# A two-layer graph attention kernel: layer 1's masks on ScalarE in two operations, and missing parts added by VectorE straight from PSUM

## The chip, the cores and the metric

The kernel runs on one core of one Trainium2 chip. The metric is the device time of one execution in microseconds. Five engines work side by side, each through its own queue in program order, and wait for one another through semaphores: TensorE (PE; its weight loads are shown as PEld), VectorE (DVE), ScalarE (ACT), GpSimd (POOL) and SyncE (SP, which here only issues DMAs).

## The reference

`x` has 6250 rows of 768 numbers; there are 100,000 edges, sorted by destination, and every node has a loop to itself. Two graph attention layers (4 heads of 64, then 1 head of 256) and a two-layer MLP stand behind a layer norm and a ReLU, with a residual:

```python
def gat_conv(x, src, dst, W, a_src, a_dst, bias, heads):
    h = (x @ W).reshape(n, heads, -1)
    alpha_s = (h * a_src[None]).sum(-1)
    alpha_d = (h * a_dst[None]).sum(-1)
    e = leaky_relu(alpha_s[src] + alpha_d[dst], 0.2)
    e = exp(e - segment_max(e, dst)[dst])
    alpha = e / (segment_sum(e, dst)[dst] + 1e-16)
    out = segment_sum(h[src] * alpha[:, :, None], dst)
    return out.reshape(n, -1) + bias
...
h = relu(gat_conv(relu(layernorm(x)), ..., heads=4))
h = relu(gat_conv(h, ..., heads=1))
return x + relu(h @ Wm1 + bm1) @ Wm2 + bm2
```

## The kernel before

The first stage (up to about 190 us) computes layer 1's features for 49 tiles of 128 nodes. Each tile stays in SBUF (`kept[t]`) and is stored as rows of `table[1]` in DRAM. Then layer 1 and layer 2 each run `layer_edges` over the edges, in `NG` = 196 groups `g` of 4 tiles of 128 edges; two tiles make a pair, 8 tiles a unit `u`, 16 tiles a node tile `t` (four groups, `j` = 0 to 3). The whole order of instructions on each engine is written out by hand in the loop over `g` (a manual schedule); there is no planner.

For a pair, GpSimd gathers the 128 source rows of each tile by an indirect DMA (L714) into a buffer `G` (24 buffers of one pair), 8 groups ahead of its use in program order. VectorE then multiplies the pair's weights (L792, L802) and, in layer 1, scales the gathered rows to `hw` (L804, 8 buffers); TensorE multiplies them by a one-hot matrix `hot` (L742, VectorE) and sums into `o_ps` (L816, one PSUM buffer for each unit). In layer 2 VectorE builds the weighted one-hot `hw` instead (L799). VectorE joins the units' sums (`acc`, L827), ScalarE copies their quarters (`sum`, L836), and the node's steps (normalise, turn, product with W2; L1010 to L1071) follow some groups later.

The weights need, for every edge, a factor of its destination node. For that a mask of 128 x 1024 bf16 is made for each unit: mask[p, e] is 1 where edge e's destination has the number p within its window of 128 nodes, else 0. `drow` holds the numbers modulo 128 on every partition; `pidx` holds p. TensorE multiplies the mask by the factors (`meet`, L760, into the one PSUM buffer `e_parts`), ScalarE copies the result (`parts_sb`, L772), and VectorE adds its three parts (`join`, L779). In layer 1 `make_mask` (L731) makes the mask on VectorE and SyncE writes it to DRAM (`mask_d`, L733); layer 2 reads it back. `make_mask` is called in the groups with odd `j`, for a unit about 5 units further on; `meet(t + 2)` is called at `j` = 0; `parts_out(t + 2)` at `j` = 3. There are 6 mask buffers.

Some pairs (30 in layer 1, one in each six or seven groups; 10 in layer 2) are gathered ahead, while the table that they read is not complete yet; sources that are not there yet are read as row 0. Such pairs (`SOON`, `NEXT`) are kept in DRAM and come back into a `G` buffer by a SyncE DMA (`soon_back`, L321). What is missing in them is added later: VectorE builds one-hot matrices of the missing sources, one for each missing node tile (`soon_hits`, L334, 3 buffers; in one to three parts, each one group before its product), TensorE multiplies them by the tiles in SBUF (`soon_missing`, L347; all into one PSUM buffer with the tag `missing`), ScalarE copies the sum to SBUF (`soon_out`, L352, tile `soon_m`), and VectorE multiplies the row by a 0/1 flag and adds the copy (`soon_whole`, L357). A pair has two tiles k; for a pair used in group `at`, the last part of its second tile is multiplied in group `at - 2`, copied in `at - 1`, and both rows are made whole in `at`. In layer 2 the same is done by `next_hits`, `next_missing` (L410), `next_out` (L416, tile `next_m`) and `next_whole` (L421): the products in `at - 6` and `at - 2`, the copies one group later, both additions in `at`.

Within a group the order is: the first pair, the node's steps, `gather_up`, `make_hot`, at fitting `j` `meet`, `ahead` or `make_mask`, then the actions on the early rows in the order of `SOON_ORDER`, then the second pair, the steps again, and at `j` = 3 `parts_out` and `join`.

Of the kernel before, what the change touches and what calls it, by code (L numbers as in the profile page):

```python
# [10 lines left out]
F32 = mybir.dt.float32  # L11
BF16 = mybir.dt.bfloat16
I32 = mybir.dt.int32
AF = mybir.ActivationFunctionType
ALU = mybir.AluOpType
AX = mybir.AxisListType

P = 128
# [44 lines left out]
def portions(there):  # L63

    n = -(-(NT - there) // PART)
    cuts = [there + (NT - there) * k // n for k in range(n + 1)]
    return list(zip(cuts, cuts[1:]))


SOON_DOES = {}  # L70
for i, at in enumerate(SOON_GROUP):
    todo = [(2 * i + t, k) for t in range(2) for k in range(len(portions(SOON[i])))]
    for j, (k, part) in enumerate(todo):
        g = at - 1 - len(todo) + j
        SOON_DOES.setdefault(g - 1, []).append(("hits", k, part))
        SOON_DOES.setdefault(g, []).append(("missing", k, part))
        if part == len(portions(SOON[i])) - 1:
            SOON_DOES.setdefault(g + 1, []).append(("out", k, part))
            SOON_DOES.setdefault(at, []).append(("whole", k, part))
    SOON_DOES.setdefault(max(at - 5 - len(todo), 0), []).append(("sources", i, 0))  # L80
SOON_ORDER = ("whole", "out", "missing", "hits", "sources")

UP_AT = {4 * u + 11: u for u in range(NU - 16)}
UP_AT.update(zip((338, 341, 344, 348, 351, 355, 358, 362, 366, 370, 373, 377, 380, 384), range(NU - 16, NU - 2)))
# [9 lines left out]
def kernel(  # L94
# [21 lines left out]
    nc = tc.nc  # L116
# [3 lines left out]
    def pool(name, bufs, **kw):  # L120
        return ctx.enter_context(tc.tile_pool(name=name, bufs=bufs, **kw))

    const = pool("const", 1)
# [4 lines left out]
    def bcast(src, n, off=0):  # L128
# [9 lines left out]
                   allow_small_or_imprecise_dtypes=True)  # L138
    pidx = const.tile([P, 1], F32, name="pidx")
    nc.gpsimd.iota(pidx, pattern=[[0, 1]], base=0, channel_multiplier=1,  # L140
                   allow_small_or_imprecise_dtypes=True)
    nid = const.tile([P, NT], F32, name="nid")
    nc.gpsimd.iota(nid, pattern=[[P, NT]], base=0, channel_multiplier=1,
                   allow_small_or_imprecise_dtypes=True)
    wbase = const.tile([P, NU, 2 * TPG], F32, name="wbase")
    nc.gpsimd.iota(wbase, pattern=[[64, NU], [0, 2 * TPG]], base=-32, channel_multiplier=0,
                   allow_small_or_imprecise_dtypes=True)
# [4 lines left out]
    nc.vector.tensor_copy(nid_ps, nid)  # L152
    eps_c = const.tile([P, 1], F32, name="eps_c")
    nc.vector.memset(eps_c, EPS)
    idle = const.tile([P, 4 * P], BF16, name="idle")
    nc.vector.memset(idle, 0.0)
    ones_c = const.tile([P, 1], F32, name="ones_c")
# [19 lines left out]
    TW = {1: RW[1] + 8, 2: RW[2] + 1}  # L177
# [113 lines left out]
    soon_i = const.tile([P, len(SOON), 2], I32, name="soon_i")  # L291
    soon_ok = const.tile([P, len(SOON), 2], F32, name="soon_ok")
    soon_d = dram.tile([len(SOON), P, 2 * TW[1]], F32, name="soon_d")
    soon_G, soon_of, soon_p, soon_hit, soon_m = {}, {}, {}, {}, {}
    soon_pair = {i: pair for pair, i in SOON_AT.items()}
    renewed = set()

# [49 lines left out]
            nc.tensor.matmul(soon_p[k], hit[:, T - a], kept[T], start=(T == there),  # L347
                             stop=(T == NT - 1))

    def soon_out(pool, k):  # L350
        soon_m[k] = pool.tile([P, TW[1]], F32, name="soon_m", bufs=3)
        nc.scalar.activation(soon_m[k], soon_p.pop(k), AF.Copy)  # L352

    def soon_whole(G, k):
        i, t = divmod(k, 2)
        row = G[soon_pair[i]][:, t]
        nc.vector.scalar_tensor_tensor(row, row, soon_ok[:, i, t:t + 1], soon_m.pop(k),  # L357
                                       ALU.mult, ALU.add)

    next_i = const.tile([P, len(NEXT), 2], I32, name="next_i")  # L360
    next_ok = const.tile([P, len(NEXT), 2], F32, name="next_ok")
    next_d = dram.tile([len(NEXT), P, 2, TW[2]], F32, name="next_d")
    next_G, next_of, next_p, next_hit, next_m = {}, {}, {}, {}, {}
    next_pair = {i: pair for pair, i in NEXT_AT.items()}

    def next_places(i):
# [24 lines left out]
    def next_sources(pool, i):  # L391

        next_of[i] = pool.tile([P, 2 * P], I32, name="next_of", bufs=1)
        nc.sync.dma_start(next_of[i], bcast(src_rows, 2 * P, 2 * P * next_pair[i]))

    def next_hits(pool, i, t):

        m = NT - NEXT[i]
        next_hit[i, t] = pool.tile([P, NT - NEXT_FROM, P], F32, name="next_hit", bufs=2)
        nc.vector.tensor_tensor(  # L400
            next_hit[i, t][:, :m],
            next_of[i][:, t * P:(t + 1) * P].unsqueeze(1).to_broadcast([P, m, P]),
            nid_ps[:, NEXT[i]:].unsqueeze(2).to_broadcast([P, m, P]), ALU.is_equal)

    def next_missing(i, t):

        there, hit = NEXT[i], next_hit.pop((i, t))
        next_p[i, t] = ps.tile([P, TW[2]], F32, name="missing2", tag="missing", bufs=1)
        for T in range(there, NT):
            nc.tensor.matmul(next_p[i, t], hit[:, T - there], kept[T][:, :TW[2]], start=(T == there),  # L410
                             stop=(T == NT - 1))

    def next_out(pool, i, t):

        next_m[i, t] = pool.tile([P, TW[2]], F32, name="next_m", bufs=2)
        nc.scalar.activation(next_m[i, t], next_p.pop((i, t)), AF.Copy)  # L416

    def next_whole(G, i, t):

        row = G[next_pair[i]][:, t]  # L420
        nc.vector.scalar_tensor_tensor(row, row, next_ok[:, i, t:t + 1], next_m.pop((i, t)),  # L421
                                       ALU.mult, ALU.add)

    def next_steps(g, pool, sm, G):

        for i, at in enumerate(NEXT_GROUP):
            if g == at - 10:
                next_sources(pool, i)
            for t in range(2):
                first = at - 6 + 4 * t  # L430
                if g == first - 1:
                    next_hits(pool, i, t)
                if g == first:
                    next_missing(i, t)
                if g == first + 1:
                    next_out(sm, i, t)
                if g == at:
                    next_whole(G, i, t)

    mask_d = dram.tile([NU * P, 8 * P], BF16, name="mask_d")  # L440
# [216 lines left out]
    drow, mask = {}, {}  # L657
# [15 lines left out]
    def fetch_mask(u):  # L673

        if u < NU:
            b = (min(8 * u + 8, LAST) - 8 * u) * P
            mask[u] = maskp.tile([P, 8 * P], BF16, name="mask")
            nc.sync.dma_start(mask[u][:, :b], mask_d[u * P:(u + 1) * P, :b])

    def layer_edges(layer, H, node, pre, matched, pre_pool):  # L680
# [4 lines left out]
        with tc.tile_pool(name=f"eg{layer}", bufs=6) as eg, \  # L685
# [33 lines left out]
            def both(u):  # L719
                return tiles(2 * u)[0], TPG + tiles(2 * u + 1)[-1] + 1  # L720

            def make_mask(u):

                if not 0 <= u < NU:
                    return
                if layer == 2:
                    return fetch_mask(u + 1)
                a, b = (t * P for t in both(u))
                mask[u] = maskp.tile([P, 8 * P], BF16, name="mask")
                at = u % 2 * 8 * P  # L730
                nc.vector.tensor_scalar(mask[u][:, a:b], drow[u // 2][:, at + a:at + b], pidx, None,  # L731
                                        ALU.is_equal)
                nc.sync.dma_start(mask_d[u * P:(u + 1) * P, a:b], mask[u][:, a:b])  # L733

            def make_hot(g):
# [138 lines left out]
            if layer == 1:  # L874
                for r in range(3):
                    fetch_rows(r)
                soon_away(0)
                fetch_rows(3)
                for u in range(4):
                    make_mask(u)  # L880
            else:
                next_away()
# [46 lines left out]
            for g in range(NG):  # L929
                t, j = divmod(g, 4)  # L930
# [21 lines left out]
                if j == 0:  # L952
                    if layer == 1:
                        fetch_rows(t + 4)
                    node.prefetch(t)
                    if layer == 2 or t == 0:
                        meet(t + 1)
                    if layer == 1 and t > 0:
                        meet(t + 2)
                elif j == (2 if t < NT - 1 else 1):  # L960
                    node.ahead(t)
                elif j % 2 and (layer == 2 or t > 0):
                    make_mask((g + (11 if layer == 1 else 7)) // 2)
# [7 lines left out]
                if layer == 1:  # L971
                    for what, k, part in sorted(SOON_DOES.get(g, ()),
                                                key=lambda d: (SOON_ORDER.index(d[0]), d[1], d[2])):
                        if what == "whole":
                            soon_whole(G, k)
                        elif what == "out":
                            soon_out(sm, k)
                        elif what == "missing":
                            soon_missing(k, part)
                        elif what == "hits":  # L980
                            soon_hits(pre_pool, k, part)
                        else:
                            soon_sources(pre_pool, k)
                else:
                    next_steps(g, pre_pool, sm, G)
# [545 lines left out]
```

## Time and profile before

| what | value |
|---|---|
| median of 3 runs | 2706.55 us (2704.31 to 2711.71) |
| profiled execution | 2711.53 us, of which 2709.7 are the span from its first to its last instruction |
| TensorE, weight loads | 1897.7 and 1425.3 us busy |
| VectorE | 1495.4 us busy |
| ScalarE | 454.4 us busy |
| GpSimd | 1534.3 us busy |
| mean granted TensorE clock | 0.821 |

Times inside the span count from its start. A group of instructions is told by its line in the kernel, engine, operation and tile (out<-in), with the number of instructions, the busy time and the mean duration; the idle time of the engine just before these instructions follows, with what released them. "Issue" is time in which the engine waited for nothing that the trace shows; "remote" and "another core or an unknown queue" are waits without a releaser in the trace. In a timeline, the columns are the start in us, the duration in us, the engine, the line, the operation, out<-in with its shape, how many instructions were merged, and in brackets the idle time before and its releaser.

### The profile page before, as it was taken

The page shows a single profiled execution, that of the slowest core. Times are in us where ns is not written, and L with a number is a line of the kernel's source. Part 1 is how long each engine was busy: PE and PEld are TensorE (multiplying, and loading weights), DVE is VectorE, ACT ScalarE, POOL GpSimd, SP SyncE. Part 2 cuts the span into 40 slices and gives each one's busy share as a digit, 9 for nine tenths or more (in the row PEclk, how much of TensorE's full clock was granted, in tenths as well). Part 3 has the DMA queues.
Part 4 walks back from the last instruction along what each step waited for, and adds up shares of the span by engine and source line. Part 5 has one row for each costly group of instructions (what it writes and reads, how often), then busy time and mean ns, then how long its engine had stood idle before and what let it go on. Part 6 is the DMA issues. An engine that isn't in the chain of part 4 may idle for free.

```text
span 2709.7 us, 28790 instructions
## 1 busy us (share of the span) xinstructions
PE 1897.7 (70%) x8572; PEld 1425.3 (53%) x8574; DVE 1495.4 (55%) x4344; ACT 454.4 (17%) x1415; POOL 1534.3 (57%) x1669
## 2 busy tenths in 40 slices
PE   9772486888796877866656436777777667777668
PEld 7651365666575655645435224555554445545445
DVE  8542476667675756565666424454544445454445
ACT  6540011111111111101102101111111111111112
POOL 5457455455554545354562466666666666666661
PEclk9985698899897888887788657888878878877779
DMA  9877344444544444343552554455545555554442
GB/s 358 247 240 240 115 140 136 125 133 141 146 128 123 135 113 139 109 128 106 147 155 68 144 148 116 140 155 154 157 146 155 155 149 155 153 158 147 143 146 92
DMA packets 174907, 405.46 MB, mean 150 GB/s; under 512 B 37192, under 2 KB 61983, under 8 KB 174743
## 3 DMA queue, kind: packets, MB, share of 16 engines
q0 software_dynamic: 75040, 210.90, 29.5%
q1 hardware_dynamic: 98332, 191.14, 20.9%
q10 hardware_dynamic: 1370, 1.48, 0.2%
q8 instruction: 72, 1.18, 0.2%
q14 instruction: 93, 0.75, 0.1%
HBM read 334.24 MB, written 69.14 MB: 149 GB/s over the span
## 4 chain that ended last, share of the span: by engine, by line
PE 37%; issue 21%; another core or an unknown queue 15%; DVE 13%; POOL 3%; DMA 2%; ACT 1%; DVEq 0%; ACTq 0%; POOLq 0%
PE o_ps L816 17%; PE missing L347 9%; PE y_ps L1186 5%; POOL G L714 3%; DVE hw L799 2%; PE missing L410 2%; DMA G<-table,src_i 2%; DVE hw L804 2%; DVE hot L742 2%; DVE soon_hit L334 1%; DVE iota_ps L792 1%; PE tp L1176 1%; DVE acc L827 1%; PE e_parts L760 1%
## 5 line engine op out<-in xcount | busy, mean ns | idle before, releaser
L714 POOL DMA_INDIRECT G<-table,src_i x1484 | 1416.8, 955 | 1053.2 <-issue 380.7
L816 PE MATMUL o_ps<-G,hw 128*128 128x258 f32 x1564 | 487.1, 446 | 177.0 <-issue 130.3
L347 PE MATMUL missing<-kept,soon_hit 128*128 128x268 f32 x1648 | 463.3, 432 | 207.7 <-ACT soon_m L352 130.5
L347 PEld LDWEIGHTS missing<-kept,soon_hit 128*128 128x128 f32 x1648 | 342.6, 212 | 301.0 <-ACT soon_m L352 138.0
L816 PEld LDWEIGHTS o_ps<-G,hw 128*128 128x128 f32 x1564 | 338.8, 223 | 299.8 <-issue 192.0
L816 PE MATMUL o_ps<-hw,hot 128*128 128x260 f32 x1564 | 413.5, 405 | 83.8 <-issue 51.7
L816 PEld LDWEIGHTS o_ps<-hw,hot 128*128 128x128 f32 x1564 | 306.8, 201 | 157.2 <-issue 61.8
L804 DVE TENSOR_TENSOR hw<-G,iota_ps 128x520 f32<-128x520 f32 x391 | 272.0, 696 | 96.6 <-PE e_parts L760 38.0
L799 DVE TENSOR_SCALAR hw<-iota_ps,dcol,w 128x128 f32<-128x128 f32 x782 | 284.9, 405 | 16.8 <-DVE w L795 2.5
L836 ACT ACTIVATE sum<-acc 32x260 f32<-32x260 f32 (+1 forms) x384 | 160.0, 417 | 592.7 <-DVE acc L827 304.2
L1190 DVE TENSOR_TENSOR y<-y_ps,xt 128x384 f32<-128x384 f32 (+1 forms) x98 | 54.4, 556 | 294.6 <-remote 106.7
L1186 PE MATMUL y_ps<-wm,mT 128*128 128x384 f32 x392 | 175.9, 577 | 31.2 <-issue 22.6
L760 PE MATMUL e_parts<-win,mask 128*128 128x12 bf16 (+1 forms) x1564 | 68.0, 167 | 171.2 <-issue 128.0
L357 DVE SCALAR_TENSOR_TENSOR G<-G,soon_ok,soon_m 128x268 f32<-128x268 f32 x60 | 29.3, 494 | 261.8 <-ACT soon_m L352 257.7
L334 DVE TENSOR_TENSOR soon_hit<-soon_of,iota_ps 128x896 f32<-128x896 int32 (+6 forms) x126 | 128.3, 1019 | 64.3 <-remote 37.2
L512 PE MATMUL h_ps<-w,r 128*128 128x264 f32 (+1 forms) x588 | 145.5, 402 | 16.2 <-ACT r L502 8.7
L760 PEld LDWEIGHTS <-mask 128*128 128x128 bf16 x1564 | 61.3, 97 | 180.4 <-issue 172.3
L792 DVE TENSOR_TENSOR iota_ps<-G,iota_ps 128x8 f32<-128x8 f32 (+1 forms) x782 | 128.7, 165 | 34.2 <-DMA G<-table,src_i 11.1
L512 PEld LDWEIGHTS h_ps<-w,r 128*128 128x128 f32 x588 | 113.2, 200 | 39.6 <-ACT r L502 10.7
L742 DVE TENSOR_TENSOR hot<-iota_ps,dcol 128x512 f32<-128x512 f32 x196 | 133.3, 681 | 0.0
L1186 PEld LDWEIGHTS y_ps<-wm,mT 128*128 128x128 f32 x392 | 75.4, 214 | 101.6 <-issue 69.1
L352 ACT ACTIVATE soon_m<-missing 128x268 f32<-128x268 f32 x60 | 23.7, 394 | 594.1 <-PE missing L347 292.2
(424 smaller groups left out, 1494.4 us busy)
## 6 DMA issues: line engine op xcount, KB each, us to landing
xt<-in_x SPq DMA_DIRECT2D x96, 384.0 KB
drow<-dmod_d SPq DMA_DIRECT2D x49, 512.0 KB
mask_d<-mask SPq DMA_DIRECT2D x97, 256.0 KB
mask<-mask_d SPq DMA_DIRECT2D x97, 256.0 KB
G<-table,src_i POOLq DMA_INDIRECT x1484
out<-y SPq DMA_DIRECT2D x48, 384.0 KB
xTt<-in_xT SPq DMA_DIRECT2D x35, 384.0 KB
soon_d<-G SPq DMA_DIRECT2D x30, 268.0 KB
```

The lines of the kernel that those rows point to most:

```text
L334: nc.vector.tensor_tensor(soon_hit[k, part][:, :b - a], soon_of[i][:, t * P:(t + 1) * P].unsqueeze(1).to_broadcast([P, b - a, P]), nid_ps[ ...
L347: nc.tensor.matmul(soon_p[k], hit[:, T - a], kept[T], start=(T == there), stop=(T == NT - 1))
L512: nc.tensor.matmul(h_ps[:, :n], r[:, k], w1[:, k, :n], start=(k == 0), stop=(k == KI - 1))
L714: nc.gpsimd.indirect_dma_start(out=G[k // 2][:n, k % 2], out_offset=None, in_=table[layer], in_offset=bass.IndirectOffsetOnAxis(ap=src_i[: ...
L742: nc.vector.tensor_tensor(hot[g][:, T[0]:T[0] + n], iota_ps.unsqueeze(1).to_broadcast([P, n, P]), dcol[:, k:k + n].unsqueeze(2).to_broadca ...
L760: nc.tensor.matmul(parts[t][:, at + k], m[:, k * P:(k + 1) * P], pre.win[:, 2 * u + 2], start=True, stop=True)
L792: nc.vector.tensor_mul(v, e2, v)
L799: nc.vector.tensor_scalar(hw[:, t], iota_ps, dcol[:, k:k + 1], w[:, t], ALU.is_equal, ALU.mult)
L804: nc.vector.tensor_mul(hw, Gp[:, :, :RW[1]].rearrange("p t (h c) -> p t h c", h=H), w.unsqueeze(3).to_broadcast([P, 2, H, C + 1]))
L816: nc.tensor.matmul(o_ps[u], l, r[:, :RW[layer]], start=(g % 2 == 0 and k == 0), stop=(g % 2 == 1 and k == tiles(g)[-1]))
L836: nc.scalar.activation(done[t][r], acc[r], AF.Copy)
L1186: nc.tensor.matmul(y_ps, mT[:, j], wm2[:, j, s * half:(s + 1) * half], start=False, stop=(j == KH - 1))
```

## The change

The mask of layer 1 is made by ScalarE: |drow - p| with a per-partition bias `less` (which holds -p), then relu(1 - that) in place, which is 1 where the two are equal and 0 elsewhere. `less` is filled once at the start by GpSimd. `soon_out` and `next_out` are gone: `soon_whole` and `next_whole` read the PSUM sum themselves. They are called one group after the last product of their tile, where the copy stood, and no longer in group `at`; among the actions of a group `whole` comes first, as before.

```diff
         if part == len(portions(SOON[i])) - 1:
-            SOON_DOES.setdefault(g + 1, []).append(("out", k, part))
-            SOON_DOES.setdefault(at, []).append(("whole", k, part))
+            SOON_DOES.setdefault(g + 1, []).append(("whole", k, part))
...
-SOON_ORDER = ("whole", "out", "missing", "hits", "sources")
+SOON_ORDER = ("whole", "missing", "hits", "sources")
...
+    less = const.tile([P, 1], F32, name="less")
+    nc.gpsimd.iota(less, pattern=[[0, 1]], base=0, channel_multiplier=-1,
+                   allow_small_or_imprecise_dtypes=True)
...
-    def soon_out(pool, k):
-        soon_m[k] = pool.tile([P, TW[1]], F32, name="soon_m", bufs=3)
-        nc.scalar.activation(soon_m[k], soon_p.pop(k), AF.Copy)
-
     def soon_whole(G, k):
         i, t = divmod(k, 2)
         row = G[soon_pair[i]][:, t]
-        nc.vector.scalar_tensor_tensor(row, row, soon_ok[:, i, t:t + 1], soon_m.pop(k),
+        nc.vector.scalar_tensor_tensor(row, row, soon_ok[:, i, t:t + 1], soon_p.pop(k),
                                        ALU.mult, ALU.add)
...
-    def next_out(pool, i, t):
-        next_m[i, t] = pool.tile([P, TW[2]], F32, name="next_m", bufs=2)
-        nc.scalar.activation(next_m[i, t], next_p.pop((i, t)), AF.Copy)
-
     def next_whole(G, i, t):
         row = G[next_pair[i]][:, t]
-        nc.vector.scalar_tensor_tensor(row, row, next_ok[:, i, t:t + 1], next_m.pop((i, t)),
+        nc.vector.scalar_tensor_tensor(row, row, next_ok[:, i, t:t + 1], next_p.pop((i, t)),
                                        ALU.mult, ALU.add)
...
                 if g == first + 1:
-                    next_out(sm, i, t)
-                if g == at:
                     next_whole(G, i, t)
...
-                nc.vector.tensor_scalar(mask[u][:, a:b], drow[u // 2][:, at + a:at + b], pidx, None,
-                                        ALU.is_equal)
+                m = mask[u][:, a:b]
+                nc.scalar.activation(m, drow[u // 2][:, at + a:at + b], AF.Abs, bias=less)
+                nc.scalar.activation(m, m, AF.Relu, scale=-1.0, bias=ones_c)
                 nc.sync.dma_start(mask_d[u * P:(u + 1) * P, a:b], mask[u][:, a:b])
```

More of the change, by code (lines that the diff above doesn't have):

```diff
@@ L293 @@
     soon_d = dram.tile([len(SOON), P, 2 * TW[1]], F32, name="soon_d")
-    soon_G, soon_of, soon_p, soon_hit, soon_m = {}, {}, {}, {}, {}
+    soon_G, soon_of, soon_p, soon_hit = {}, {}, {}, {}
     soon_pair = {i: pair for pair, i in SOON_AT.items()}
@@ L362 @@
     next_d = dram.tile([len(NEXT), P, 2, TW[2]], F32, name="next_d")
-    next_G, next_of, next_p, next_hit, next_m = {}, {}, {}, {}, {}
+    next_G, next_of, next_p, next_hit = {}, {}, {}, {}
     next_pair = {i: pair for pair, i in NEXT_AT.items()}
```

## The prediction

> **What bounds the kernel now.** I read the engines' totals first, then the waits, then the chain by stages, then two stretches instruction by instruction. Totals and waits of the whole run:
>
> ```profile
> span 2709.7 us, 28790 instructions
> PE 1897.7 (70%) x8572; PEld 1425.3 (53%) x8574; DVE 1495.4 (55%) x4344; ACT 454.4 (17%) x1415; POOL 1534.3 (57%) x1669
> ...
> DVE G L357 <- ACT soon_m L352: 257.7, 27, 18.7
> ...
> ACT soon_m L352 <- remote: 230.9, 15, 26.4
> ...
> PE missing L347 <- ACT soon_m L352: 130.5, 13, 20.3
> ```
>
> No engine is full; three wait for one another. The copy soon_m (ScalarE, L352) sits in the middle: TensorE waits 130.5 us for it (13 times, it frees the one PSUM buffer of the missing parts), VectorE 257.7 us (27 times). "Remote" means that the trace shows nobody who released it. By stages, layer 1 (200 to 1500 us) and layer 2, and the chain where layer 1 runs well:
>
> ```profile
> 200.00:1500.00 1300.00, 903.49 (x4237) 717.05 (x4238) 805.63 (x2022) 163.68 (x566) 684.43 (x715) 0.83 0.47 133
> 1500.00:2709.00 1209.00, 831.84 (x3610) 577.11 (x3609) 569.71 (x2017) 180.00 (x491) 745.49 (x783) 0.79 0.50 146
> ...
> by line: PE missing L347 56.6%; PE o_ps L816 29.2%; issue 7.5%; PE h_ps L1063 4.4%; PE e_parts L760 1.9%; PE tp L1010 0.7%
> ```
>
> The last row is the chain from 640 to 700 us: TensorE is the bound there, and VectorE's masks cost nothing. But over the 1300 us TensorE works only 903. The missing 400 us lie in stalls, of two kinds. The first, on the timeline:
>
> ```profile
> 453.89 2.96 PE L347 MATMUL missing<-kept,soon_hit 128*128 128x268 f32 x12
> 471.69 0.69 DVE L804 TENSOR_TENSOR hw<-G,iota_ps 128x520 f32<-128x520 f32 x1 [0.60 <-DVE iota_ps L802]
> 474.64 0.95 POOL L714 DMA_INDIRECT G<-table,src_i  x1 [0.30 <-issue]
> 479.33 0.39 ACT L352 ACTIVATE soon_m<-missing 128x268 f32<-128x268 f32 x1 [26.43 <-remote]
> 479.75 0.50 DVE L357 SCALAR_TENSOR_TENSOR G<-G,soon_ok,soon_m 128x268 f32<-128x268 f32 x1 [6.77 <-ACT soon_m L352]
> 479.77 2.60 PE L347 MATMUL missing<-kept,soon_hit 128*128 128x268 f32 x5 [20.30 <-ACT soon_m L352]
> ```
>
> TensorE's products end at 456.8; the copy that needs them starts 22 us later; VectorE runs on until it needs the copy; GpSimd, gathering one tile each 0.95 + 0.30 = 1.25 us, ends at 475.6; 3.7 us after that everything moves again. The second kind:
>
> ```profile
> 823.65 0.17 PE L760 MATMUL e_parts<-win,mask 128*128 128x12 bf16 x1 [3.33 <-issue]
> 828.58 0.94 POOL L714 DMA_INDIRECT G<-table,src_i  x1 [0.30 <-issue]
> 832.79 4.28 PE L347 MATMUL missing<-kept,soon_hit 128*128 128x268 f32 x11 [0.80 <-issue]
> 842.90 0.39 ACT L352 ACTIVATE soon_m<-missing 128x268 f32<-128x268 f32 x1 [22.60 <-PE missing L347]
> 843.33 0.50 DVE L357 SCALAR_TENSOR_TENSOR G<-G,soon_ok,soon_m 128x268 f32<-128x268 f32 x1 [18.38 <-ACT soon_m L352]
> 848.04 0.95 POOL L714 DMA_INDIRECT G<-table,src_i  x1 [18.51 <-DVE hw L804]
> ```
>
> TensorE crawls ("issue", 3.33 us before a 0.17 us product) while gathers run, and is back at full rate 3.3 us after the last one ends at 829.5. GpSimd stops only because VectorE, held at L357, frees no more G buffers. So in both kinds the order is: VectorE stops, GpSimd fills its 24 buffers and stops, 3 to 4 us later the stall is over. That a stall ends because the gathers pause is my reading of the order; the trace does not name it.
>
> **The change part by part.** Prices:
>
> ```profile
> L731 DVE TENSOR_SCALAR mask<-drow,pidx x98: 409/475/685, 197.9 to 1457.8; 128x1024 bf16<-128x1024 bf16 x97, 128x768 bf16<-128x768 bf16 x1
> L264 ACT ACTIVATE drm<-dri 98x1024 bf16<-98x1024 int32 x1 | 1.0, 1042 | 0.0
> L517 ACT ACTIVATE kept<-h_ps,rstd 128x256 f32<-128x256 f32 x49 | 23.1, 472 | 58.2 <-PE h_ps L512 38.0 <-remote 12.5 <-issue 5.5
> L1067 ACT ACTIVATE kept<-h_ps 128x256 f32<-128x256 f32 x49 | 18.5, 378 | 88.5 <-remote 51.5 <-PE h_ps L1063 33.2 <-PE missing L347 3.8
> L827 DVE SCALAR_TENSOR_TENSOR acc<-acc,keep,o_ps 128x260 f32<-128x260 f32 x94 | 44.8, 476 | 0.0
> L357 DVE SCALAR_TENSOR_TENSOR G<-G,soon_ok,soon_m 128x268 f32<-128x268 f32 x60 | 29.3, 494 | 261.8 <-ACT soon_m L352 257.7 <-issue 4.1
> L352 ACT ACTIVATE soon_m<-missing x60: 394/394/396, 322.0 to 1485.7; 128x268 f32<-128x268 f32 x60
> L742 DVE TENSOR_TENSOR hot<-iota_ps,dcol 128x512 f32<-128x512 f32 x193 | 131.6, 682 | 0.0
> by line: issue 23.7%; PE missing L347 19.7%; another core or an unknown queue 18.3%; PE o_ps L816 9.9%; POOL G L714 5.7%; DVE hw L804 3.2%; DVE hot L742 3.2%; DVE soon_hit L334 2.7%; DMA G<-table,src_i 2.6%; DVE iota_ps L802 1.7%; DVE iota_
> ```
>
> (a) Masks leave VectorE: 98 x 475 ns = 46.6 us. The last row is the chain from 195 to 1500 us: of hot (L742), issued beside the masks, 3.2% of 1305 = 41.8 us lie on the chain out of 131.6 busy, 32%. The same share of the masks is 15 us. Bounds 0 and 46.6; I take -15.
>
> (b) Masks on ScalarE. A 1024-wide operation took 1042 ns; a per-partition operand adds 472 - 378 = 94, so 1.14 us each, 2.27 a mask, 98 x 2.27 = 222 us, on an engine busy 164 of 1300 us. It fits. What matters is what queues behind: the sums' copies, rT, and every second time parts_sb, which frees TensorE's buffer for the next e_parts one group later. Of these 48 places TensorE pays 0 to 2.27 us, 0 to 109 in all. In even running ScalarE has a group (1300 us / 196 = 6.6 us) in hand and pays nothing; after a stall all wait for ScalarE's backlog. I take ten stalls: +22. SyncE's mask_d writes wait longer too, and behind them in its queue stand drow, soon_of and the returning G rows:
>
> ```profile
> 655.87 0.43 SPq L321 DMA_DIRECT2D G<-soon_d  x1
> 699.38 0.55 DVE L357 SCALAR_TENSOR_TENSOR G<-G,soon_ok,soon_m 128x268 f32<-128x268 f32 x1
> ```
>
> These rows are issued 43.5 us ahead of their use. The first addition now comes up to four groups (26 us) earlier; 17 us remain, seven masks' worth, so I cost it at nothing; without that cover VectorE would wait for the row as long as the write is late.
>
> The Trainium skill speaks against this move: "ScalarE: Activation LUTs", Rules for kernel authors, gives relu and adding to VectorE, up to about 3x faster in bf16; our rows make it 475 against some 2270 ns. By its formula, 280 ns + 0.833 per element and 93 of overlap, I estimate 2.17 us a mask, 213 in all: the same sum.
>
> (c) soon_m goes, 60 copies of 394 ns; L357 reads PSUM itself. L827 does that in 476 ns, L357 took 494 from SBUF: no dearer. TensorE's next missing part now waits 494 instead of 394 ns: 60 x 0.1 = +6 where nothing covers it.
>
> (d) The 130.5 us that TensorE waited for the copy. VectorE needs the same signal from TensorE that the copy needed, so the late start can stay. But VectorE now stops there itself: between 457 and 473 us it would free no G, and GpSimd would end up to 16 us sooner. Bounds 0 (the signal is late whatever waits) and -130 (nothing is late). Nearest is the mean wait, 10 us, half the one shown, with fewer hw tiles ready for TensorE after it; I take a quarter, -33. Next late then is parts_sb or rT on ScalarE.
>
> (e) Each pair's second addition moves one group earlier, from `at` to `at`-1. VectorE stops a group sooner, GpSimd four gathers (5 us) sooner; against it TensorE finds one group less prepared. Over 27 waits that is 0 to -135; I take half a microsecond each, -13.
>
> (f) Behind the waiting addition stand, on VectorE, the hits of the next group (1.08 us for seven tiles) and the group's second pair (0.17 + 0.17 + 0.70): with the addition 2.6 us until TensorE gets its next pair. TensorE meanwhile has 8 products of o_ps (1.92) and 12 of missing (2.88), as quoted next. Covered with 2 us to spare; where a part has only four products the cover is about gone.
>
> ```profile
> 811.52 1.08 DVE L334 TENSOR_TENSOR soon_hit<-soon_of,iota_ps 128x896 f32<-128x896 int32 x1
> 812.10 2.88 PE L347 MATMUL missing<-kept,soon_hit 128*128 128x268 f32 x12
> 814.81 1.92 PE L816 MATMUL o_ps<-hw,hot 128*128 128x260 f32 x8
> ```
>
> (g) Start of layer 1: four masks before the first parts_sb, 9.1 instead of 1.9 us, so 7 later; but VectorE then waits for gathers anyway, and an 8.38 us wait of VectorE for a free mask buffer moves to ScalarE. Bounds -8 and +7; 0.
>
> ```profile
> 212.49 0.17 DVE L792 TENSOR_TENSOR iota_ps<-G,iota_ps 128x8 f32<-128x8 f32 x1 [1.68 <-DMA G<-table,src_i]
> 222.91 0.65 DVE L731 TENSOR_SCALAR mask<-drow,pidx 128x1024 bf16<-128x1024 bf16 x1 [8.38 <-issue]
> ```
>
> (h) Layer 2: 20 copies go; VectorE is tied to TensorE's products within one group instead of two or more.
>
> ```profile
> DVE G L421 <- ACT next_m L416: 16.0, 1, 16.0
> ```
>
> It waited there once in 20, so it is rarely two groups ahead; idle half the time, it catches up. 0, bounds -7 and +20.
>
> Sum: -15 + 22 + 6 - 33 - 13 = -33. The profiled execution took 2711.5 us (span 2709.7), 5 over the median 2706.55; 2711.5 - 33 = 2678.5, as a median 2673.
>
> **The rivals.** *The stall moves* (no change): the late signal is as late for VectorE, (d) and (e) give nothing, and as the stalls stay as long, half of (b) runs inside them: -15 + 11 + 6 = +2, 2708. For it: "remote" names nobody, so ScalarE may be innocent. *Slower, ScalarE's queue*: the mask ahead of parts_sb is late at half of the 48 places, +54, and only (a) comes back: 2706 + 39 = 2745. It decides from the point where ScalarE reaches parts_sb over 6.6 us after VectorE has done the same group. For it: stalls leave backlogs. Against: TensorE waited for parts_sb once. *Slower, VectorE tied*: the cover of (f) fails at 60 places by 0.5 us and (d), (e) give nothing: 2706 + 30 - 15 + 6 = 2727. *Much faster*: half of (d) and a third of (e), -65 and -45, ScalarE hidden, -15 + 6: 2587. *The change fails to do what it says*: Abs is new here.
>
> ```profile
> L133 ACT ACT_TABLE_LOAD x1 | 1.3, 1283 | 0.6 <-PEq L1522 0.6
> ```
>
> If Abs and Exp shared no table, two loads of 1283 ns a mask, 251 us on ScalarE, would push the time past 2800. The Trainium skill, same page, Table sets, says that abs and relu are in every set; no run here shows Abs yet.
>
> **How the numbers follow.** Forecast 0.43, stall moves 0.18, ScalarE's queue 0.15, VectorE tied 0.10, much faster 0.13, table 0.01. A measurement tells 0.3%, 8 us. Faster 0.43 + 0.13 = 0.56, same 0.18, slower 0.26. The range leaves out the table, half of the queue case and half of the much faster one: 2605 to 2738. The forecast's own range is 2640 to 2698.
>
> **What would show it.** Two ACT rows of about 1.14 us, 98 each, and no soon_m row; missing (L347) waiting for DVE G instead; GpSimd's pauses as many but shorter, TensorE's idle time in layer 1 below 400 us by some 30. I am wrong if missing waits as long for DVE G as for soon_m, or if e_parts begins to wait for mask or parts_sb.

## The result and the profile after

| | before | after |
|---|---|---|
| median, 4 runs each | 2707.75 us | 2662.84 us (2657.62 to 2665.92) |
| profiled execution (span) | 2711.53 us (2709.7) | 2657.62 us (2655.5) |

The ratio is 0.9832, 95% interval [0.9809, 0.9854]: 45 us faster, where 33 were forecast. The engines' totals after, the two layers as windows (columns: window, its length, busy us and instructions of PE, PEld, DVE, ACT, POOL, then the clock, DMA share, GB/s), and two of the waits:

```profile
span 2655.5 us, 28661 instructions
PE 1917.6 (72%) x8572; PEld 1426.7 (54%) x8574; DVE 1456.2 (55%) x4246; ACT 638.7 (24%) x1531; POOL 1528.3 (58%) x1670
...
200.00:1500.00 1300.00, 954.68 (x4318) 735.40 (x4319) 786.09 (x1991) 358.82 (x733) 709.95 (x747) 0.84 0.48 139
1500.00:2655.00 1155.00, 804.28 (x3520) 562.66 (x3520) 550.39 (x1950) 165.76 (x437) 714.37 (x752) 0.81 0.49 146
...
DVE G L355 <- PE missing L349: 183.5, 23, 13.9
...
DVE G L355 <- remote: 106.0, 19, 8.0
```

From 200 to 1500 us TensorE now works 955 instead of 903 us: 51 us less idle, and layer 1 ends that much sooner. (The new kernel has reached layer 2 before 1500, so the two windows do not hold the same work.) VectorE's work fell by 39 us, ScalarE's rose by 184. The groups of the operations that the change touched (count, busy us, mean ns, then the engine's idle time before them and what ended it):

```profile
L723 ACT ACTIVATE mask<-drow,less 128x1024 bf16<-128x1024 bf16 x98 | 112.3, 1146 | 0.0
L724 ACT ACTIVATE mask<-mask,ones_c 128x1024 bf16<-128x1024 bf16 x98 | 112.3, 1146 | 3.2
L132 ACT ACT_TABLE_LOAD x1 | 1.3, 1283 | 0.6 <-PEq L1514 0.6
L355 DVE SCALAR_TENSOR_TENSOR G<-G,soon_ok,missing 128x268 f32<-128x268 f32 x60 | 29.6, 493 | 333.4 <-PE missing L349 183.5 <-remote 106.0 <-PE h_ps L1055 17.1
L349 PE MATMUL missing<-kept,soon_hit 128*128 128x268 f32 x1648 | 448.4, 420 | 75.1 <-issue 59.0 <-DVE G L355 14.9
L808 PE MATMUL o_ps<-hw,hot 128*128 128x260 f32 x1564 | 456.9, 430 | 159.3 <-issue 108.7 <-DVE hw L796 42.3 <-DVE iota_ps L794 3.8
L752 PE MATMUL e_parts<-win,mask 128*128 128x12 bf16 (+1 forms) x1564 | 68.5, 167 | 168.2 <-issue 127.2 <-ACT parts_sb L764 30.3 <-DVE win L636 6.0
```

The same rows of the kernel before:

```profile
L347 PE MATMUL missing<-kept,soon_hit 128*128 128x268 f32 x1648 | 463.3, 432 | 207.7 <-ACT soon_m L352 130.5 <-issue 76.6
L816 PE MATMUL o_ps<-hw,hot 128*128 128x260 f32 x1564 | 413.5, 405 | 83.8 <-issue 51.7 <-DVE hw L804 19.2 <-DVE iota_ps L792 8.5
L760 PE MATMUL e_parts<-win,mask 128*128 128x12 bf16 (+1 forms) x1564 | 68.0, 167 | 171.2 <-issue 128.0 <-ACT parts_sb L772 35.5 <-DMA G<-table,src_i 3.8
```

TensorE's idle time ahead of the missing parts falls from 207.7 to 75.1 us, 133 less. Ahead of o_ps it rises from 83.8 to 159.3, 75 more: hw keeps it waiting longer (19.2 to 42.3), and the idle time that the trace gives no cause for ("issue") doubles (51.7 to 108.7). The whole account, from the first to the last of VectorE's 391 layer-1 products hw: 1312 us before, 1255 after. TensorE's idle time in that stretch falls by 86 us (397 to 311), and its busy time rises by 30 (915 to 944; one product of o_ps takes 430 ns instead of 405, and no run shows why). Where the 57 us arise is seen from the times at which VectorE has finished the n-th of these products (worked out from the timelines):

```
pair          0     60    120    180    200    240    280    320    390
before    202.7  442.4  634.5  818.3  893.5 1030.9 1168.2 1320.9 1514.9
after     207.0  434.5  635.3  823.6  891.3 1011.6 1134.4 1268.5 1462.2
```

Nothing is gained up to pair 200; then 50 us between pairs 200 and 320. In layer 2 the lead stays between 49 and 55. VectorE's waits at the addition were looked at next. For the first 30 and then the last 30 of the 60 additions, first in the kernel before, then in the kernel after (us, times):

```profile
  ACT soon_m L352: 92.0, 10
  issue: 3.5, 4
...
  ACT soon_m L352: 165.7, 17
  issue: 0.6, 1
```

```profile
  PE missing L349: 93.2, 11
  remote: 57.1, 11
  PE o_ps L808: 9.9, 2
...
  PE missing L349: 90.3, 12
  remote: 48.9, 8
  PE h_ps L1055: 11.7, 2
```

In the first half VectorE waits 172 us in all (with the small rows left out here) instead of 95. In the second half it waits 162 instead of 166, but in more and shorter pieces. A pair has two tiles, and the timelines part their additions. At the first tile's, which before stood two to four groups behind its copy, VectorE waited 19 us in the first half and 26 in the second; now it waits 99 and 106, because each addition is tied to a product only one group ahead of it. At the second tile's it waited 77 and 141 us, and now 72 and 56. So the tie costs 80 us of waiting in either half, and only in the second half is as much saved at the second tiles. That fits where the time is gained; that it is the reason is not shown, for waits of VectorE are not time of the kernel. One stall of the second half, before and after (the 36th addition of both):

```profile
1007.87 0.50 DVE L357 SCALAR_TENSOR_TENSOR G<-G,soon_ok,soon_m 128x268 f32<-128x268 f32 x1 [18.69 <-ACT soon_m L352]
1011.46 0.95 POOL L714 DMA_INDIRECT G<-table,src_i  x1 [18.47 <-DVE iota_ps L779]
```

```profile
980.32 0.49 DVE L355 SCALAR_TENSOR_TENSOR G<-G,soon_ok,missing 128x268 f32<-128x268 f32 x1 [7.84 <-PE missing L349]
982.10 0.95 POOL L705 DMA_INDIRECT G<-table,src_i  x1 [4.49 <-DVE iota_ps L784]
```

One wait of 18.7 us became one of 7.8 (the pair's other addition now waits 3.8, and did not before), and GpSimd's pause behind it 4.5 instead of 18.5. Counted over layer 1, GpSimd's pauses above 6 us went from 19 with 247 us to 16 with 165. Each kernel has one more at the end of the layer, 47.3 us before and 35.8 after.

### The profile page after: what moved, and what is told of

Read it like the earlier page. It is cut to its first block, busy times and chain, and to the rows that moved or that the text cites. A ratio compares the mean times of both kernels' runs of the same rounds, so it can differ in the third digit from the quotient of the medians.

```text
span 2655.5 us, 28661 instructions
## 1 busy us (share of the span) xinstructions
PE 1917.6 (72%) x8572; PEld 1426.7 (54%) x8574; DVE 1456.2 (55%) x4246; ACT 638.7 (24%) x1531; POOL 1528.3 (58%) x1670
## 4 chain that ended last, share of the span: by engine, by line
PE 41%; issue 20%; DVE 18%; another core or an unknown queue 14%; POOL 2%; DMA 2%; ACT 2%; SPq 0%; DVEq 0%; ACTq 0%; POOLq 0%
PE o_ps L808 17%; PE missing L349 10%; PE y_ps L1178 4%; PE h_ps L503 4%; DVE hw L796 3%; DVE hw L791 2%; POOL G L705 2%; DVE hot L734 2%; PE missing L408 2%; DVE iota_ps L784 2%; DVE soon_hit L336 2%; DVE iota_ps L794 1%; DMA G<-table,src_i 1%; DVE acc L819 1%
## 5 line engine op out<-in xcount | busy, mean ns | idle before, releaser
L808 PE MATMUL o_ps<-hw,hot 128*128 128x260 f32 x1564 | 456.9, 430 | 159.3 <-issue 108.7
L349 PE MATMUL missing<-kept,soon_hit 128*128 128x268 f32 x1648 | 448.4, 420 | 75.1 <-issue 59.0
L808 PEld LDWEIGHTS o_ps<-hw,hot 128*128 128x128 f32 x1564 | 322.2, 212 | 260.7 <-issue 131.0
L349 PEld LDWEIGHTS missing<-kept,soon_hit 128*128 128x128 f32 x1648 | 330.6, 205 | 160.4 <-issue 81.7
L355 DVE SCALAR_TENSOR_TENSOR G<-G,soon_ok,missing 128x268 f32<-128x268 f32 x60 | 29.6, 493 | 333.4 <-PE missing L349 183.5
L1178 PE MATMUL y_ps<-wm,mT 128*128 128x384 f32 x392 | 168.2, 554 | 18.5 <-issue 13.1
L1173 ACT ACTIVATE mT<-tp,bm1c 128x128 f32<-128x128 f32 x98 | 30.7, 364 | 426.0 <-remote 220.9
```

The source lines that it names most:

```text
L808: nc.tensor.matmul(o_ps[u], l, r[:, :RW[layer]], start=(g % 2 == 0 and k == 0), stop=(g % 2 == 1 and k == tiles(g)[-1]))
L1178: nc.tensor.matmul(y_ps, mT[:, j], wm2[:, j, s * half:(s + 1) * half], start=False, stop=(j == KH - 1))
```

## The experiments

The kernels were measured in five groups, each beside the kernel before on the same chip. The groups fell into two kinds, and the kernel before, unchanged, came in both. In two of them (and in the first measurement) the kernel before took 2677 to 2708 us, and the traces taken there show the stalls described. In three it took 2082 to 2085 us; it was not profiled there itself, but the traces of the kernels beside it show no such stall. Below, "with stalls" and "without stalls" stand for these two kinds. So each result is read against the kernel before of its own group. Three theories were to be told apart, lettered here as in the later expectations. A: VectorE is stopped a group sooner, it stops GpSimd sooner, and the stalls end sooner. B: the 47 us of masks that leave VectorE count. C: the copy leaves TensorE's path.

| kernel | before of its group | kernel | ratio, 95% |
|---|---|---|---|
| after_again | 2677.26 | 2628.25 | 0.9822 [0.9804, 0.9840] |
| psum_l1 | 2678.47 | 2616.66 | 0.9780 [0.9747, 0.9813] |
| masks_act | 2082.41 | 2077.24 | 0.9974 [0.9965, 0.9982] |
| masks_twice | 2082.41 | 2108.76 | 1.0119 [1.0105, 1.0133] |
| add_psum | 2082.41 | 2106.96 | 1.0114 [1.0099, 1.0129] |
| early_add | 2082.41 | 2126.27 | 1.0209 [1.0195, 1.0222] |
| masks_act_b | 2083.06 | 2077.96 | 0.9980 [0.9970, 0.9989] |
| add_psum_b | 2083.06 | 2104.16 | 1.0100 [1.0080, 1.0119] |
| early_add_b | 2083.06 | 2125.07 | 1.0200 [1.0178, 1.0221] |
| after_third | 2083.06 | 2097.12 | 1.0075 [1.0053, 1.0098] |
| add_psum_c | 2084.58 | 2105.45 | 1.0113 [1.0085, 1.0141] |

before_again, a profile of the kernel before in the group of after_again, took 2676.12 us.

**The masks alone** (masks_act). The kernel before with only this edit:

```diff
-                nc.vector.tensor_scalar(mask[u][:, a:b], drow[u // 2][:, at + a:at + b], pidx, None,
-                                        ALU.is_equal)
+                m = mask[u][:, a:b]
+                nc.scalar.activation(m, drow[u // 2][:, at + a:at + b], AF.Abs, bias=less)
+                nc.scalar.activation(m, m, AF.Relu, scale=-1.0, bias=ones_c)
```

> Only the masks move to ScalarE; the copies soon_m and next_m and the late additions stay as before. Theory A (the additions straight from PSUM, one group earlier, shorten layer 1's stalls): no gain, 2700 to 2730, since ScalarE gets 222 us of work ahead of a copy that TensorE waits for. Theory B (VectorE's relief of 47 us is what counts, in the second half of layer 1): most of the 45 us, 2665 to 2680. Theory C (the copy leaves TensorE's path): no gain or a loss, 2705 to 2740.

**The additions alone** (add_psum): the diff of the change without the hunk above.

> Only the additions change: straight from PSUM, one group after the last product, in both layers; the masks stay on VectorE. Theory A (VectorE stops a group sooner): most of the 45 us, 2660 to 2685. Theory B (relief by the masks): 2700 to 2715. Theory C (no copy between TensorE and its next missing part): 2660 to 2685 as well; early_add tells A from C.

**The early addition with the copy kept** (early_add):

```diff
-            SOON_DOES.setdefault(at, []).append(("whole", k, part))
+            SOON_DOES.setdefault(g + 1, []).append(("whole", k, part))
...
-SOON_ORDER = ("whole", "out", "missing", "hits", "sources")
+SOON_ORDER = ("out", "whole", "missing", "hits", "sources")
```

with the same in layer 2.

> The kernel before with the ScalarE copies kept, but VectorE adds each copy in the group in which it is made, as early as in the changed kernel; masks on VectorE. Theory A: like add_psum, 2660 to 2690, as VectorE is tied to TensorE in the same way. Theory C: like the kernel before, 2700 to 2715, as TensorE still waits for the copy. Theory B: 2700 to 2715.

**Every mask made twice on VectorE** (masks_twice): the line of the mask stands there a second time.

> The kernel before with every mask of layer 1 made twice on VectorE, 98 more operations of 475 ns, 47 us. Theory B: VectorE's masks lie on the path, so +30 to +45, 2735 to 2755. Theories A and C: a third of them at most is on the path (the share that I took in the prediction), 0 to +15, 2705 to 2722.

These four ran without stalls, so none of the three theories of the gain was tested, and the picture was the reverse of the first measurement's. The masks alone gained 5 us, the additions alone lost 24, the early additions behind a copy lost 44, and doubled masks lost 26 for 47 us of VectorE work. The waits of three of them from 200 to 1100 us (waiter, what it waited for: us, times, longest); first the masks alone, then the additions alone, then the early addition with its copy:

```profile
PE o_ps L820 <- DVE hw L808: 50.0, 46, 3.6
DVE G L360 <- ACT soon_m L355: 25.7, 13, 4.0
```

```profile
PE o_ps L807 <- DVE hw L795: 72.6, 69, 8.4
DVE G L355 <- PE missing L349: 57.5, 33, 3.7
```

```profile
PE o_ps L815 <- DVE hw L803: 75.7, 86, 3.0
DVE G L357 <- ACT soon_m L352: 67.0, 37, 3.6
```

Where nothing stalls, work added to VectorE counts: 26 of 47 us, 56%, came out as time. Work taken from it counts less: the same 47 us gained 5, with TensorE busy for 839 of layer 1's 902 us in masks_act, and 61 of the other 63 us spent waiting for hw (worked out from the timeline). The early addition makes VectorE wait for products that the late one finds finished (57.5 against 25.7 us), and TensorE then waits for hw (72.6 against 50.0). These two kernels differ in their masks as well; after_third below has the masks of masks_act and the early additions, and shows the same: VectorE waits 78.9 us instead of 25.7, and TensorE waits for hw 65.2 instead of 50.0. That is the rival "VectorE tied", which the prediction priced at 0.5 us for each of 60 additions, 30 us. The copy costs another 19 to 21 us when the early addition stands right behind it (early_add against add_psum, in both groups). TensorE does not wait for the copy there; VectorE does (67.0 against 57.5).

**The change and the kernel before once more** (after_again, before_again).

> The changed kernel once more, beside the kernel before, on the chip of the last four runs, where the kernel before takes 2082 us and GpSimd has no pause over 6 us. If the parts add up as they measured there (masks -0.26%, additions +1.14%): +0.9%, about 2101 us. If the two help each other, since the relief on VectorE pays for its earlier waits: 2070 to 2085. Theory A (the change shortens stalls) has no stalls to shorten there and expects no gain; should the chip be one with stalls (the kernel before at about 2708), A expects the first result again, 2655 to 2670.

> The kernel before, unchanged, for a profile on the same chip as the experiments: about 2082 us there, TensorE idle between 200 and 1100 us for less than 15% and no pause of GpSimd over 6 us; or about 2708 us with the stalls of the first profile, if they come with the kernel and not with the chip.

Here the kernel before stalled again. The change gained 48 us [43, 52], and the windows from 880 to 1440 us of before_again and after_again show where: in the same 560 us TensorE issues 1919 instead of 1772 matmuls.

```profile
880.00:1440.00 560.00, 380.81 (x1772) 300.51 (x1770) 344.33 (x888) 72.42 (x251) 296.25 (x310) 0.82 0.45 129
```

```profile
880.00:1440.00 560.00, 429.80 (x1919) 323.90 (x1918) 371.56 (x973) 167.31 (x363) 301.02 (x317) 0.87 0.46 132
```

**The parts and the whole on one chip** (masks_act_b, add_psum_b, early_add_b, after_third; the same edits, and the change itself).

> The masks alone on ScalarE; copies of the missing parts and late additions as in the kernel before. Three theories. A: VectorE, stopped a group sooner by the addition, ends the stalls sooner, and the masks matter little. B: the 47 us that VectorE no longer spends on masks are what counts, in the second half of layer 1. C: TensorE's wait for ScalarE's copy was the loss. On a chip with stalls (the kernel before at 2675 to 2710 us): A expects 0 to -10 us, B expects -30 to -50 us, all of it after pair 200, and C expects a slower kernel, 0 to +20 us, because the copies queue behind the masks on ScalarE and TensorE goes on waiting for soon_m. On a chip without stalls (before at about 2080) all three expect the -5 us measured there.

> The additions alone straight from PSUM, one group after the last product; the masks stay on VectorE. Theories as for the masks alone: A (VectorE is stopped sooner, the stalls end sooner), B (the masks' relief), C (the copy leaves TensorE's path). On a chip with stalls: A and C expect -35 to -50 us, most of the whole change's -45 to -49; B expects 0 to +25 us, as the tie cost +24 us on the chip without stalls and nothing pays it back. TensorE's row of waits for soon_m is gone in either case. On a chip without stalls: +24 us again.

> The kernel before with the copies kept and each addition moved into the group of its copy: VectorE is stopped as early as in the changed kernel, but TensorE still waits for ScalarE's copy. On a chip with stalls: A expects -25 to -50 us, since only the time at which VectorE stops counts; C expects 0 to +40 us, since the copy is still on TensorE's path; B expects +20 to +44 us, as on the chip without stalls. On a chip without stalls: +44 us again.

> The whole change once more, beside its parts on one chip. On a chip with stalls -45 to -49 us by the two measurements so far. If the parts are independent, it is the sum of the masks alone and the additions alone, within 8 us; if the masks' relief pays only where VectorE is tied to the products, it is lower than the sum by 10 us or more. On a chip without stalls no run shows the whole change yet: the parts' sum gives -5 + 24 = +19 us, 2101; with the relief paying back what the tie costs (56% of 47 us, from the doubled masks, is 26), -2 us, about 2080.

Again without stalls. The parts repeat: -5, +21, +42 us. The whole change, measured without stalls for the first time, is slower: +14 us, ratio 1.0075 [1.0053, 1.0098]. The parts add up, -5 + 21 = +16. The expectation that the relief of the masks pays back what the tie costs (-2 us) failed: with the early additions the masks' move gains 7 us (2097.12 against 2104.16), without them 5. Layer 1 of the whole change (after_third), by its stages and waits:

```profile
195.00:850.00 655.00, 620.39 (x3144) 509.63 (x3143) 542.50 (x1333) 241.64 (x477) 494.26 (x522) 0.97 0.64 187
...
PE o_ps L808 <- DVE hw L796: 65.2, 71, 3.0
DVE G L355 <- PE missing L349: 78.9, 39, 4.1
```

The same window of the first measurement's kernel after has 482 us of TensorE's work, 2228 matmuls and a clock of 0.84:

```profile
195.00:850.00 655.00, 481.91 (x2228) 376.06 (x2229) 385.28 (x938) 182.27 (x339) 369.52 (x390) 0.84 0.50 148
```

Without stalls TensorE is busy 95% of that window, so little is left to gain at its waits.

**The additions alone, a third time** (add_psum_c); whether a gain shows depends on whether the kernel before stalls beside it.

> The additions alone straight from PSUM, the masks on VectorE, to be had beside a kernel before that stalls (2675 to 2710 us). There: A (VectorE is stopped sooner and the stalls end sooner) and C (the copy leaves TensorE's path) expect -35 to -55 us, nearly all of it between pairs 200 and 360, and no row of TensorE waiting for soon_m; B (the masks' relief counts) expects -10 to +25 us and a progress that falls behind. If masks and additions add up as they do without stalls, the masks alone are then worth the whole change's -47 less this number. Beside a kernel before without stalls (2080 us): +21 to +24 us again, and the cause of the gain stays open.

There were none: 2105.45 against 2084.58 us, +21 again. It repeats the cost of the tie and says nothing of the gain.

**The additions from PSUM in layer 1 alone** (psum_l1): masks on VectorE, layer 2 with its copies.

```diff
-            SOON_DOES.setdefault(g + 1, []).append(("out", k, part))
-            SOON_DOES.setdefault(at, []).append(("whole", k, part))
+            SOON_DOES.setdefault(g + 1, []).append(("whole", k, part))
...
-        nc.vector.scalar_tensor_tensor(row, row, soon_ok[:, i, t:t + 1], soon_m.pop(k),
+        nc.vector.scalar_tensor_tensor(row, row, soon_ok[:, i, t:t + 1], soon_p.pop(k),
```

> The additions straight from PSUM in layer 1 alone; layer 2 keeps its copies, and the masks stay on VectorE (the column less is filled but not used). Beside a kernel before that stalls (2675 to 2710 us): A (VectorE is stopped sooner and the stalls end sooner) and C (the copy leaves TensorE's path) expect -35 to -55 us, between pairs 200 and 360; B (the masks' relief counts) expects -10 to +25 us. Beside a kernel before without stalls (2080 us), where both layers together cost +21 to +24 us: if the tie in layer 1 is the whole cost, +20 to +30 us; if layer 2's half of the change costs something too, less than +15 us.

Here the kernel before took 2678 us, the kind with stalls, and the changed one had the lowest ratio of all: 0.978 [0.9747, 0.9813], -59 us with the interval -68 to -50. Its window from 880 to 1440 us and its rows of the additions and of TensorE's missing parts:

```profile
880.00:1440.00 560.00, 433.25 (x1925) 329.20 (x1923) 388.13 (x1015) 76.62 (x283) 308.30 (x321) 0.87 0.47 132
...
L355 DVE SCALAR_TENSOR_TENSOR G<-G,soon_ok,missing 128x268 f32<-128x268 f32 x60 | 29.5, 492 | 269.6 <-PE missing L349 154.4 <-remote 70.8 <-PE h_ps L1061 22.3
L349 PE MATMUL missing<-kept,soon_hit 128*128 128x268 f32 x1648 | 446.9, 420 | 75.5 <-issue 51.2 <-DVE G L355 23.5
```

TensorE issues 1925 matmuls in the window where the whole change issued 1919, with the masks still on VectorE. So B falls: the additions in layer 1 alone bring the whole gain. In the whole change VectorE waits longer at the additions (316.7 us in after_again, against 269.6 here). The rest of the change, masks and layer 2 together, is worth -48 - (-59) = +11 us, with an interval of about +1 to +21 (two groups on two chips, whose kernels before differ by 1.2 us); by this it takes back a little of the gain. The traces part it further. From the last hw of layer 1 to the last of layer 2, before_again, after_again and psum_l1 take 1163.6, 1163.2 and 1162.4 us, so layer 2's half of the change brings and costs nothing that shows. The profiled executions of after_again and psum_l1 differ by 6 us, 3.5 of them before layer 1's first hw and 2 from there to its last. So with stalls the masks' move brings nothing that shows, and costs little. The masks alone were not measured with stalls.

A and C are not separated, so what ends the stalls sooner stays open. Both expect what psum_l1 did; early_add would tell them apart with stalls, and neither of its two groups had any. What the traces show fits both: TensorE's 130.5 us of waits for soon_m are gone (C), and GpSimd's pauses are shorter (A).

## Why the prediction was right, step by step

The forecast was 2673 us, faster; 2662.84 was measured, inside its own range of 2640 to 2698. The part that was to bring the gain, the additions in layer 1, did bring it. Its size was off, one cover that was taken for granted failed, and of the two ways in which the gain was to come, (d) and (e), the runs do not say which it was. That the measurement came out with stalls was luck for the sign: without them the same change is slower.

- (a), (b), masks: -15 and +22 were taken, together +7. With layer 2 at 0 the runs give +11 [+1, +21] with stalls. The sum fits; the split was not measured, but (a) was taken from hot's share of the chain, and psum_l1 issues as many matmuls without that relief, so its -15 is not to be seen. The price was right: two operations of 1146 ns, 2.29 us against 2.27, 225 against 222 us. By the formula of the Trainium skill, "ScalarE: Activation LUTs", section "What ACT_TABLE_LOAD costs", 280 ns + 0.833 per element, one such operation is estimated at 1133 ns; the 1146 measured agree within 13 ns. The 93 ns of overlap between two operations, which the prediction took from the same section of the Trainium skill, is not seen here: the second operation reads what the first one writes, and starts some 33 ns after its end. TensorE's waits for parts_sb did not grow: they cost e_parts 30.3 us after, 35.5 before.
- The move took 475 ns a mask from VectorE and put two operations of 1146 ns on ScalarE. Without stalls it gained 5 us all the same, where 61 of TensorE's 63 idle us in layer 1 were waits for VectorE's hw; with stalls nothing shows that it paid. An operation's price on one engine against the other does not decide it. The rule of the Trainium skill, "ScalarE: Activation LUTs", section "Rules for kernel authors", that relu and add belong on VectorE, compares such prices; the trace agrees that VectorE is the cheaper, 475 against 2292 ns.
- (c) +6: the direct addition takes 493 ns from PSUM against 494 from SBUF, as priced. TensorE waits for it (DVE G) 14.9 us, more than the 6 reckoned.
- (d) -33 and (e) -13, with (c) -40 in sum, measured -59 [-68, -50] with psum_l1. This is the term that was mis-sized. A quarter of TensorE's 130.5 us was taken; all of that row went, and over half of what was saved ahead of the missing parts came back ahead of o_ps (83.8 to 159.3 us). The prediction named parts_sb or rT as next late; it was the supply of hw and instructions that waited for nothing visible ("issue", 51.7 to 108.7).
- (f) VectorE tied, costed at nothing, "covered with 2 us to spare". This step failed: without stalls the tie costs 21 to 24 us. With stalls VectorE waits 205 us at the first tiles' additions instead of 45; (e) reckoned only with the second addition's move by one group, and the first one's move by up to four groups has no term but this cover. What that cost in time with stalls no run parts from the gain; it lies inside the -59.
- (g) start, 0 between -8 and +7: pair 0 comes 4.2 us later in the first measurement, 0.5 in after_again, inside the bounds. (h) layer 2, 0: the lead changes little from pair 0 to pair 781 (49 to 55 us), though VectorE's waits at the addition there grew from 16.0 to 110 us in all, the largest row being

```profile
DVE G L414 <- PE o_ps L808: 32.3, 5, 9.1
```

- Of the rivals, "the table" fell by the one ACT_TABLE_LOAD in the whole profile, and "ScalarE's queue" by the parts_sb row. "The stall moves" fell by the 59 us of psum_l1. "Much faster" had the right sign and too large a price. "VectorE tied" is what happens where nothing stalls; the prediction was argued from one profile with stalls and could not see that its sign hangs on them.
- Of the signs named, the two rows of 1.14 us, the missing row of soon_m and the shorter pauses came as written (16 instead of 19), and TensorE's idle time between 200 and 1500 us fell by 51 us instead of 30. Missing waits 14.9 us for DVE G, not 130.5 as for soon_m. That e_parts begins to wait for mask, named as a sign of being wrong, came in small: 1.8 us, and 9.6 in after_again.

## What to carry to other kernels

Ask for whom a wait is early or late before shortening it: the earlier additions take 59 us off where the kernel stalls (layer 1's alone) and add 21 to 24 where TensorE is fed almost without pause (both layers'). Relief of an engine is worth only what the engines behind it can use; VectorE lost 39 us of work here and waited longer for products. Measure the parts of a change apart: here one part carried all of the gain and the other added none to it, and the version with the first part alone (layer 1's additions from PSUM, masks on VectorE) had the lowest ratio with stalls, while masks_act, the other part alone, was the only one that gained without them.

## What was not expected of the hardware

The same kernel, unchanged, took 2707.75, 2677.26 and 2678.47 us in three measurements and 2082.41, 2083.06 and 2084.58 in three others, the quicker three within 0.2% of one another. The chip's number does not tell the kinds apart: number 7 had 2677 in one group and 2083 in another. The change itself, profiled in both (after and after_third), has the same matmuls and bytes, and GpSimd's gathers take 0.95 us in both. In the slower kind TensorE's clock is 0.82 instead of 0.92 (the kernel before). GpSimd's pauses above 6 us inside layer 1 sum to 231 us (before_again), and the kernels profiled in the quicker kind have none, but for one of at most 27 us at the end of the layer, where before_again has 47. Of TensorE's idle time in layer 1, 219 of 311 us in after are "issue", in which it waited for nothing that the trace names; in after_third it is idle for 75 us, and none of them are "issue". The chain that ended last, after in the first measurement and after_third:

```profile
PE 41%; issue 20%; DVE 18%; another core or an unknown queue 14%; POOL 2%; DMA 2%; ACT 2%; SPq 0%; DVEq 0%; ACTq 0%; POOLq 0%
```

```profile
PE 47%; DMA 20%; DVE 15%; issue 10%; POOL 7%; ACT 0%; SPq 0%; DVEq 0%; POOLq 0%; ACTq 0%
```

"Issue" and waits for an unknown queue hold 34% of the one chain, and "issue" 10% of the other. What makes the difference stays open, and with it whether, and why, the stalls end because the gathers pause.
